# A selective scan on one Trainium2 core: state sums and gate one unit later, softplus operations behind the products, a third buffer for the scan's output

## The chip, the core and the metric

The kernel runs on one core of a Trainium2 chip. The core has five engines that take their instructions in order, each from a queue of its own: PE (matrix products into PSUM), DVE (vector), ACT (activation functions), POOL (GpSimd, vector operations on SBUF alone here) and SP, which in this stage issues the DMA transfers. An instruction starts when those ahead of it on its engine are out of the way and the semaphores that it waits for have come. The metric is the device time of one execution in microseconds (us); the median of several executions counts.

## The reference

A tensor of 2 x 192 x 96 x 96 floats goes through four layers, each of the form x + layer(groupnorm(x)). The change touches the last, a selective state-space scan over 9216 positions of each of the two images, with 384 inner channels and 16 states per channel:

```python
xz = x_flat @ W_in.T
x_in, z_gate = jnp.split(xz, 2, axis=-1)
x_conv = jax.nn.silu(conv4(x_in) + conv_b)          # a causal filter of 4 taps per channel
dt, B_ssm, C_ssm = jnp.split(einsum('bdl,kd->blk', x_conv, W_x), ...)
delta = jax.nn.softplus(dt @ W_dt.T + b_dt + b_dt)
A = -jnp.exp(A_log)
def step(h, inp):
    u_t, d_t, B_t, C_t = inp
    dA = jnp.exp(d_t[..., None] * A)
    h = dA * h + (d_t * u_t)[..., None] * B_t[:, None, :]
    y_t = jnp.einsum('bdn,bn->bd', h, C_t)
    return (h, y_t)
y = (ys + D * x_conv) * jax.nn.silu(z_gate)
out = x + einsum('bdl,cd->bcl', y, W_out)
```

(`conv4` stands for the grouped convolution; the rest is cut.)

## The kernel before

The last layer is the function `layer3`; it takes the last 3.2 ms of the span. The positions of an image are cut into **steps**: 17 of 511 positions (called whole) and two of 265 and 264, 19 per image and 38 in all. The 384 channels x 16 states of a step are worked on in 12 **units**, called q0 to q11 here: three blocks of 128 channels (i) by four groups of 32 channels (v), a unit being 32 channels x 16 states in a tile of 128 partitions x 4 rows. In the profile's terms, unit k of a whole step is made of these operations:

- SP loads `bu` (L2336, 1022 KB, delta times u, repeated over the states) from a DRAM buffer `ud`; ACT copies the state into its column 0 (L2340).
- POOL multiplies `bu` by the B row (`times_b`, L2346).
- PE spreads delta over the states into four PSUM banks `da` (`steps_of`, L2356), ACT makes exp(A * delta) of each in place (`decay`, L2370). There are five such banks, so that only one of the next unit's four can be filled before the present scan has let go of the others.
- DVE runs the recurrence, four scans into `h` (`scan`, L2379); ACT keeps the last column (`keep`, L2386).
- Products with the C row: DVE does three of the four rows of `h` into `hc` (`times_c`, L2403), POOL the fourth into `hp` (`times_c_aside`, L2414).
- PE adds the 16 states up in a PSUM bank `acc` (`sum_of`, L2427). The first unit of every four starts the bank with D times u (the `skip` product, L2421), and after the fourth DVE multiplies by the gate (`gate`, L2440, into `y`), which frees the one `acc` bank.

Work for coming steps is put between the units by generators that advance at set places. `early(s + 2)` projects (L2242), filters (L2262) and activates; it starts in q3, does its first product in q5 and its last in q10, and SiLU on ACT in q11. `late(s + 1)` makes B, C and delta: product L2278 in q0, L2303 in q1 and q2, softplus as |.|, exp, +1 and log on ACT with one subtraction on DVE (L2313, with the log L2314 in q4) and three operations on POOL: L2316 in q5, L2318 in q6, L2320 in q7. L2320 makes `du`, which four DMAs (L2322) write to `ud`, from which all twelve `bu` of the next step are loaded. `output(s - 1)` (L2452, L2460) fills q3 to q5. All these products go through one PSUM bank `pe`, so each waits until the one before has been copied out.

The order on PE, ACT, DVE and POOL is that of the loop `for k in range(nk)` (L2496), written out by hand; only SP's queue is put in order by the compiler's scheduler. In an iteration k PE gets: products of a generator that runs ahead (q1, q7, q8, q9), `sum_of(k - 2)`, `steps_of(k + 1)`, products of a generator that runs behind. ACT: `decay(k + 1)`, the copies of those products, the state copies. DVE: `scan(k)`, additions of `output`, `times_c(k)`, `gate(k - 2)`, the softplus subtraction. POOL: the softplus operation if there is one, `times_c_aside(k - 1)`, `times_b(k + 2)`. SP: among others `load(k + 3)`.

Buffers: `bu` has four; `hc`, `hp`, `us` and `zs` three (pool `s3`); `h`, `xt`, `dl` and the rows of B and C two (pool `sb`); `xn`, `xi`, `du`, `ln`, `y`, `xr` one (pool `s1`). Tile waits are put in by the framework: with two buffers `scan(k)` waits until all readers of `h` of unit k - 2 are done.

Of the kernel before, what the change touches and what calls it, by code (L numbers as in the profile page):

```python
# [6 lines left out]
F32 = mybir.dt.float32  # L7
# [11 lines left out]
P = 128  # L19
CH = 96  # L20
# [38 lines left out]
def halves(ap):  # L59

    return ap.rearrange("(k p) t -> p k t", k=2)


class Net:
# [2021 lines left out]
    def layer3(self, x, out, stats):  # L2086
# [4 lines left out]
        TM = 511  # L2091
# [4 lines left out]
        NV = 4  # L2096
# [3 lines left out]
        with ExitStack() as ctx:  # L2100
            wp = ctx.enter_context(tc.tile_pool(name="w3", bufs=1))
            s1 = ctx.enter_context(tc.tile_pool(name="l3s", bufs=1))
            sb = ctx.enter_context(tc.tile_pool(name="l3", bufs=2))
            s3 = ctx.enter_context(tc.tile_pool(name="l3h", bufs=3))
# [102 lines left out]
            steps = []  # L2207
# [8 lines left out]
            def bank(T):  # L2216
                return ps.tile([P, TM], F32, name="pe")[:, :T]

            def early(s):

                b, t0, T = steps[s]
                xt = sb.tile([CH, 2, TM], F32, name="xt")[:, :, :T]
                nc.sync.dma_start(out=xt, in_=halves(x[b])[:, :, t0 : t0 + T])
                xn = s1.tile([CH, 2, TM], F32, name="xn")[:, :, :T]
                gs, gb = gns[b]
                for k in range(2):
                    nc.scalar.activation(
                        xn[:, k], xt[:, k], AF.Identity, bias=gb[:, k : k + 1], scale=gs[:, k : k + 1]
                    )
                us = s3.tile([P, ND, TM], F32, name="us")[:, :, :T]  # L2230
                zs = s3.tile([P, ND, TM], F32, name="zs")[:, :, :T]
                xi = s1.tile([P, ND, TM + 3], F32, name="xi")[:, :, : T + 3]
                got[s] = {"us": us, "zs": zs}
                if t0 == 0:
                    nc.gpsimd.memset(tail, 0.0)
                nc.scalar.copy(xi[:, :, 0:3], tail)
                yield

                def project(at):
                    pe = bank(T)  # L2240
                    for k in range(2):
                        nc.tensor.matmul(  # L2242
                            pe, w_in[:, k, at : at + P], xn[:, k], start=k == 0, stop=k == 1
                        )
                    return pe

                for d in range(ND):
                    pe = project(d * P)
                    yield
                    nc.scalar.copy(xi[:, d, 3:], pe)  # L2250
                    if d == ND - 1:
                        nc.scalar.copy(tail, xi[:, :, T : T + 3])
                    yield
                for d in range(ND):
                    pe = project(DI + d * P)
                    yield
                    nc.scalar.copy(zs[:, d], pe)  # L2257
                    yield
                for d in range(ND):
                    pe = bank(T)  # L2260
                    for j in range(4):
                        nc.tensor.matmul(  # L2262
                            pe, taps[:, d, j], xi[:, d, j : j + T], start=j == 0, stop=j == 3
                        )
                    yield
                    nc.scalar.activation(us[:, d], pe, AF.Identity, bias=cb[:, d : d + 1])
                    yield
                nc.scalar.activation(zs, zs, AF.Silu)
                nc.scalar.activation(us, us, AF.Silu)
                yield  # L2270
# [57 lines left out]
            def where(k):  # L2328
                return k // NQ, k % NQ, k % NQ // NV, k % NV
# [13 lines left out]
            def times_b(k):  # L2343
                s, q, _, _ = where(k)
                bu = got[s]["bu", q][:, :, 1:]
                nc.gpsimd.tensor_tensor(  # L2346
                    bu, bu, got[s]["bs"].unsqueeze(1).to_broadcast([P, 4, steps[s][2]]), ALU.mult
                )
# [17 lines left out]
            def decay(k):  # L2366
                s, q, _, _ = where(k)
                for r in range(4):
                    da = got[s]["da", q][r][:, 1:]
                    nc.scalar.activation(  # L2370
                        da, da, AF.Exp, scale=nA[:, 4 * q + r : 4 * q + r + 1]
                    )

            def scan(k):
                s, q, _, _ = where(k)
                h = sb.tile([P, 4, TM + 1], F32, name="h")[:, :, : steps[s][2] + 1]
                bu = got[s]["bu", q]
                for r in range(4):
                    nc.vector.tensor_tensor_scan(  # L2379
                        h[:, r], got[s]["da", q][r], bu[:, r], 0.0, ALU.mult, ALU.add  # L2380
                    )
                got[s]["h", q] = h
# [5 lines left out]
            def rows_c(s):  # L2388
                cc = ps.tile([P, TM], F32, name="cc")[:, : steps[s][2]]
                nc.tensor.matmul(  # L2390
                    cc,
                    pick.rearrange("p n e -> p (n e)"),
                    got[s]["xd"][:NST],
                    start=True,
                    stop=True,
                )
                got[s]["cc"] = cc
# [19 lines left out]
            def sum_of(k):  # L2417
                s, q, i, v = where(k)
                if v == 0:
                    acc = ps.tile([P, TM], F32, name="acc")[:, : steps[s][2]]  # L2420
                    nc.tensor.matmul(  # L2421
                        acc, skip[:, i], got[s]["us"][:, i], start=True, stop=False
                    )
                    got[s]["acc"] = acc
                acc = got[s]["acc"]
                for r in range(4):
                    nc.tensor.matmul(  # L2427
                        acc[32 * r : 32 * r + 32],
                        gather[:, v],
                        got[s]["hc", q][:, r] if r < 3 else got[s]["hp", q],  # L2430
                        start=False,
                        stop=v == NV - 1,
                        tile_position=(0, 32 * r),
                    )

            def gate(k):
                s, q, i, v = where(k)
                if i == 0:
                    got[s]["y"] = s1.tile([P, ND, TM], F32, name="y")[:, :, : steps[s][2]]
                nc.vector.tensor_tensor(  # L2440
                    got[s]["y"][:, i], got[s]["acc"], got[s]["zs"][:, i], ALU.mult
                )
# [26 lines left out]
            nk = ns * NQ  # L2469
# [23 lines left out]
            def go(name):  # L2493
                next(running[name], None)

            for k in range(nk):  # L2496
                s, q, _, _ = where(k)
                if q == 0 and s + 1 < ns:
                    running["late"] = late(s + 1)
                if q == 2 and s:  # L2500
                    running["out"] = output(s - 1)
                if q == 3 and s + 2 < ns:
                    running["early"] = early(s + 2)
                if q in AHEAD:
                    go(AHEAD[q])
                    go(AHEAD[q])
                if k >= 2:
                    sum_of(k - 2)
                if q == 0 and s:
                    rows_c(s)  # L2510
                scan(k)
                if q in (4, 5):
                    go("out")
                if k + 1 < nk:
                    steps_of(k + 1)
                if q in BEHIND:
                    go(BEHIND[q])
                if k + 1 < nk:
                    decay(k + 1)
                if q in BEHIND and BEHIND[q] != "out":  # L2520
                    go(BEHIND[q])
                if q == 3:
                    go("late")
                    go("early")
                times_c(k)
                if k >= 2 and (k - 2) % NV == NV - 1:
                    gate(k - 2)
                if q in (4, 5, 6, 7):
                    go("late")
                if q == 11:  # L2530
                    go("early")
                if k:
                    times_c_aside(k - 1)
                if k + 2 < nk:
                    times_b(k + 2)
                if k + 3 < nk:
                    load(k + 3)
                keep(k)
            sum_of(nk - 2)
            times_c_aside(nk - 1)  # L2540
            sum_of(nk - 1)
            gate(nk - 1)
            for _ in output(ns - 1):
                pass
# [93 lines left out]
```

## Time and profile before

| what | value |
|---|---|
| median of 3 runs | 10368.99 us (10358.51 to 10370.72) |
| the profiled execution | 10352.81 us |
| its span in the trace | 10351.0 us |
| mean granted PE clock over the span | 0.915 |
| one whole step (q0 to q0, first start of L2403) | 86.28, 89.68 and 87.22 us (three in a row, from 9029.57 us on) |
| busy in the first of these three | PE 81.08, DVE 78.62, POOL 79.71, ACT 54.90 us |
| first and last L2403 of the layer | 7139.6 and, in the last step's first unit, 10300.4 us |

Busy time is the time in which an engine has an instruction in execution; for PE it contains waits in its pipeline, and matmuls that run side by side in different quarters of the array overlap. A line of the waits view reads: engine and line that waited, what it waited for, total us, times, longest. In a timeline each row is one group of instructions: start, duration, engine, line, operation, and in brackets the idle time ahead of it with what ended it. "x4" is four instructions merged in one row.

### The profile page before, as it was taken

How to read it: one execution, taken by the hardware profiler on the slowest of the kernel's cores; microseconds unless marked ns; L12 is line 12 of the kernel's file. 1: busy time of each engine (PE TensorE's matmuls, PEld its weight loads, DVE VectorE, ACT ScalarE, POOL GpSimd, SP SyncE). 2: the span in 40 equal slices, each digit the busy share in tenths (PEclk: the TensorE clock that was granted, in tenths of full speed). 3: DMA queues.
4: the chain of work that ended last, by engine and by line, in shares of the span. 5: the costliest groups of instructions: out<-in, count | busy, mean ns of one | idle time of the engine just before them, and what ended most of it. 6: DMA issues, size and time to landing. Idle time of an engine off the chain costs nothing. (4 is left out here: it accounts for less than half of the span.)

```text
span 10351.0 us, 222379 instructions
## 1 busy us (share of the span) xinstructions
PE 9158.5 (88%) x87686; PEld 5342.5 (52%) x87686; DVE 8210.6 (79%) x8842; ACT 6081.6 (59%) x11850; POOL 6980.6 (67%) x5645
## 2 busy tenths in 40 slices
PE   4799999999979999999866777887999999999998
PEld 3587788787768888888722222223222222222223
DVE  5688878788677777777655789984889888888888
ACT  0366666666667677777500168664666666666665
POOL 1466666766666666666511268773888889988898
PEclk8899999999989999999978788887999999988898
DMA  8455555555434555555444344433787777878776
GB/s 148 91 139 135 136 136 139 137 136 134 119 90 128 136 136 138 139 137 138 109 131 129 117 149 159 130 118 83 172 176 172 172 174 173 173 173 172 174 170 149
DMA packets 877164, 1465.17 MB, mean 142 GB/s; under 512 B 251616, under 2 KB 682276, under 8 KB 875012
## 3 DMA queue, kind: packets, MB, share of 16 engines
q1 hardware_dynamic: 663276, 1264.09, 48.9%
q0 software_dynamic: 104000, 133.19, 5.8%
q10 hardware_dynamic: 108840, 53.57, 2.1%
q8 instruction: 701, 11.49, 0.5%
q14 instruction: 347, 2.84, 0.1%
HBM read 871.06 MB, written 381.46 MB: 121 GB/s over the span
## 5 line engine op out<-in xcount | busy, mean ns | idle before, releaser
L2379 DVE TENSOR_TENSOR_SCAN h<-da,bu 128x512 f32<-128x512 f32 (+2 forms) x1824 | 1981.6, 1148 | 374.0 <-POOL hp L2414 200.1
L581 DVE TENSOR_TENSOR sp<-h 128x2304 f32<-128x2304 f32 x790 | 2165.0, 2773 | 41.6 <-ACT h L560 41.6
L2346 POOL TENSOR_TENSOR bu<-bu,bs 128x2044 f32<-128x2044 f32 (+2 forms) x456 | 1958.3, 4295 | 66.0 <-DMA bu<-ud 53.0
L605 ACT COPY st<-pt 128x512 f32<-128x512 f32 (+1 forms) x2370 | 1213.6, 515 | 1100.8 <-PE pt L597 1029.4
L597 PE MATMUL pt<-ident,sp 128*128 128x128 f32 x14220 | 1674.8, 276 | 87.4 <-DVE sp L581 41.0
L603 DVE COPY st<-pt 128x512 f32<-128x512 f32 x1580 | 1063.7, 687 | 829.9 <-PE pt L597 810.7
L597 PEld LDWEIGHTS pt<-ident,sp 128*128 128x128 f32 x14220 | 1565.3, 142 | 169.9 <-issue 97.2
L551 POOL TENSOR_TENSOR h<-u,step 128x1152 f32<-128x1152 f32 (+1 forms) x474 | 1096.0, 2330 | 679.8 <-DVE u L524 480.8
L569 POOL DMA_DIRECT2D xw<-xp_d x2500 | 1389.9, 619 | 194.7 <-PE pt L648 82.5
L2370 ACT ACTIVATE da<-da,nA 128x511 f32<-128x511 f32 (+2 forms) x1824 | 1063.4, 638 | 595.0 <-PE da L2356 586.9
L648 PE MATMUL pt<-st,xw 64*32 64x288 f32 (+1 forms) x30000 | 1098.0, 371 | 141.8 <-DVE st L603 62.7
L674 ACT COPY val<-pt 128x288 f32<-128x288 f32 (+1 forms) x3000 | 958.0, 404 | 285.2 <-PE pt L648 259.9
L776 PE MATMUL pf<-main,wd 126*64 126x128 f32 (+1 forms) x17064 | 986.2, 274 | 9.7 <-DMA far_m<-val 9.4
L776 PEld LDWEIGHTS pf<-main,wd 126*64 126x64 f32 x17064 | 913.7, 140 | 155.9 <-issue 146.9
L2356 PE MATMUL da<-dl,spread 32*128 32x511 f32 (+2 forms) x3648 | 984.0, 643 | 6.7 <-DVE h L2379 6.7
L648 PEld LDWEIGHTS pt<-st,xw 64*32 64x32 f32 x30000 | 548.0, 107 | 556.6 <-ACT val L674 171.7
L2403 DVE TENSOR_TENSOR hc<-h,cc 128x1533 f32<-128x1533 f32 (+2 forms) x456 | 751.2, 1647 | 0.0
L797 PE MATMUL pf<-more,wl 118*64 118x144 f32 (+5 forms) x11592 | 737.9, 278 | 3.0 <-DMA more<-far_l 2.2
L797 PEld LDWEIGHTS pf<-more,wl 118*64 118x64 f32 (+1 forms) x11592 | 670.2, 137 | 71.1 <-issue 63.4
L2356 PEld LDWEIGHTS da<-dl,spread 32*128 32x128 f32 x3648 | 311.6, 192 | 674.7 <-DVE h L2379 396.1
L2414 POOL TENSOR_TENSOR hp<-h,cs 128x511 f32<-128x511 f32 (+2 forms) x456 | 553.4, 1214 | 99.6 <-DVE h L2379 48.1
L2242 PE MATMUL pe<-xn,sb_w_in 96*128 96x511 f32 (+2 forms) x912 | 527.1, 709 | 94.6 <-ACT xi L2250 37.1
(344 smaller groups left out, 13016.1 us busy)
## 6 DMA issues: line engine op xcount, KB each, us to landing
bu<-ud SPq DMA_DIRECT2D x408, 1022.0 KB
main<-val SPq DMA_DIRECT2D x2016, 91.1 KB
far_l<-val SPq DMA_DIRECT2D x288, 324.0 KB
xw<-xp_d POOLq DMA_DIRECT2D x2500, 26.0 KB
far_m<-val SPq DMA_DIRECT2D x288, 162.0 KB
half_d<-hv SPq DMA_DIRECT2D x54, 768.0 KB
hv<-half_d SPq DMA_DIRECT2D x54, 768.0 KB
more<-far_l SPq DMA_DIRECT2D x576, 60.8 KB
```

Source lines behind the costliest of these rows:

```text
L551: nc.gpsimd.tensor_tensor(hs, u[:, :, 8 * KK * l : 8 * KK * l + n].unsqueeze(3).to_broadcast([P, 2, n, WS]), con["step"].unsqueeze(1).unsq ...
L569: nc.gpsimd.dma_start(out=xw[e * WN : (e + 1) * WN, i], in_=xp_d[y : y + WS, x : x + WS, e * CM // 2 : e * CM // 2 + XW],)
L581: nc.vector.tensor_tensor(sp.rearrange("p s (y x) -> p s y x", x=WS), hy.unsqueeze(3).to_broadcast([P, n, WS, WS]), hx.unsqueeze(2).to_bro ...
L597: nc.tensor.transpose(pt[:, q], sp[:, 2 * (q0 + q) : 2 * (q0 + q) + 2].rearrange("p e w -> p (e w)"), self.ident,)
L603: nc.vector.tensor_copy(st[:, q0 : q0 + m], pt[:, :m])
L605: nc.scalar.copy(st[:, q0 : q0 + m], pt[:, :m])
L648: nc.tensor.matmul(to, xw[e * WN : (e + 1) * WN, win, g * CG : g * CG + 32], sts[pair][e * WN : (e + 1) * WN].rearrange("p s (r c) -> p s ...
L776: nc.tensor.matmul(place(cv, m, 2 - t // 3, 2 - t % 3, None, 0), con["wd"][:, cv, t, m * CO : (m + 1) * CO], blocks(took, 1, rows), start= ...
L797: nc.tensor.matmul(place(cv, m, 2 * cv if alone else 1 - cv, 2 - t, h, 1 - alone,), con["wl"][lanes, slot, t, m * CO : (m + 1) * CO], bloc ...
L2346: nc.gpsimd.tensor_tensor(bu, bu, got[s]["bs"].unsqueeze(1).to_broadcast([P, 4, steps[s][2]]), ALU.mult)
L2356: nc.tensor.matmul(das[r][:, 1:], spread[at, v].rearrange("p n e -> p (n e)"), got[s]["dl"][at, i], start=True, stop=True, tile_position=( ...
L2379: nc.vector.tensor_tensor_scan(h[:, r], got[s]["da", q][r], bu[:, r], 0.0, ALU.mult, ALU.add)
```

## The change

Four edits, all in `layer3`:

1. `h` comes from the pool with three buffers, `xt` (a step's input tile) from the pool with one.
2. `sum_of` is called for unit k - 3 and no longer for k - 2, at the same place of the iteration; at the end the last three units are summed after the loop.
3. `gate` goes with it: it is called for k - 3, so in q2, q6 and q10 instead of q1, q5 and q9. The `skip` product, which belongs to `sum_of`, moves from q2, q6, q10 to q3, q7, q11.
4. In q5, q6 and q7 the generator `late` advances after `times_c_aside(k - 1)` and `times_b(k + 2)`, no longer ahead of them. What is issued there is L2316, L2318 and L2320 on POOL and the four DMAs to `ud`. In q4 it stays where it was.

On SP, the scheduler's order differs in one place: the load of `xr` (L2448), which stood two `bu` loads behind the `ud` writes, now stands just ahead of them; the writes stand between the same two `bu` loads (of units q10 and q11) in both kernels.

```diff
-                xt = sb.tile([CH, 2, TM], F32, name="xt")[:, :, :T]
+                xt = s1.tile([CH, 2, TM], F32, name="xt")[:, :, :T]
...
-                h = sb.tile([P, 4, TM + 1], F32, name="h")[:, :, : steps[s][2] + 1]
+                h = s3.tile([P, 4, TM + 1], F32, name="h")[:, :, : steps[s][2] + 1]
...
-                if k >= 2:
-                    sum_of(k - 2)
+                if k >= 3:
+                    sum_of(k - 3)
...
                 times_c(k)
-                if k >= 2 and (k - 2) % NV == NV - 1:
-                    gate(k - 2)
-                if q in (4, 5, 6, 7):
+                if k >= 3 and (k - 3) % NV == NV - 1:
+                    gate(k - 3)
+                if q == 4:
                     go("late")
                 if q == 11:
                     go("early")
                 if k:
                     times_c_aside(k - 1)
                 if k + 2 < nk:
                     times_b(k + 2)
+                if q in (5, 6, 7):
+                    go("late")
                 if k + 3 < nk:
                     load(k + 3)
                 keep(k)
-            sum_of(nk - 2)
             times_c_aside(nk - 1)
-            sum_of(nk - 1)
+            for k in range(nk - 3, nk):
+                sum_of(k)
             gate(nk - 1)
```

## The prediction, made before the changed kernel had run

> **What bounds the kernel now.** I read the busy times of whole steps first, then the waits of the last layer, then the timelines of three consecutive steps, A (from 9029.57 us), B (from 9115.85) and C (from 9205.53). The steps repeat with lengths near 86.3, 89.7 and 86.9 us, mean 87.6. In each, DVE works 78.6 to 78.9 us, so about 9 us of a step are DVE idle time; that is all there is to gain. The last whole step, which prepares nothing for a successor, takes 78.2 us: DVE alone. The waits of the layer (waiter, releaser, total, times, longest):
>
> ```profile
> POOL ln L2316 <- ACT bu L2340: 217.6, 36, 8.4
> ...
> DVE h L2379 <- POOL hp L2414: 194.0, 86, 4.0
> ...
> DVE h L2379 <- ACT da L2370: 128.1, 133, 4.4
> ```
>
> The second line is the scan waiting for its buffer, which POOL still reads for `hp`; over the 36 steps with softplus work, 5.4 us each. The third is the scan waiting for decays. POOL's timeline in step A shows where the second comes from (L2346 is `bu` of q6, then softplus, `hp` of q4, `bu` of q7, softplus, `hp` of q5):
>
> ```profile
> 9052.49 4.52 POOL L2346 TENSOR_TENSOR bu<-bu,bs 128x2044 f32<-128x2044 f32 x1 [0.79 <-ACT du L2310]
> 9062.12 3.42 POOL L2316 TENSOR_TENSOR ln<-ln,du 128x1533 f32<-128x1533 f32 x1 [5.12 <-ACT bu L2340]
> 9065.49 1.28 POOL L2414 TENSOR_TENSOR hp<-h,cs 128x511 f32<-128x511 f32 x1
> 9066.72 4.51 POOL L2346 TENSOR_TENSOR bu<-bu,bs 128x2044 f32<-128x2044 f32 x1
> 9071.18 3.44 POOL L2318 TENSOR_TENSOR dl<-dl,ln 128x1533 f32<-128x1533 f32 x1
> 9074.57 1.27 POOL L2414 TENSOR_TENSOR hp<-h,cs 128x511 f32<-128x511 f32 x1
> ```
>
> POOL stands idle 5.12 us for the logarithm (ACT ends L2314 at 9062.04) with `hp` of q4 queued behind. That unit's scan ended at 9056.40. From there POOL needs 3.4 + 1.2 + 4.5 = 9.1 us a unit against 6.1 of DVE, and the scans of q7 and q8 start when `hp` ends:
>
> ```profile
> 9075.88 4.57 DVE L2379 TENSOR_TENSOR_SCAN h<-da,bu 128x512 f32<-128x512 f32 x4 [2.14 <-POOL hp L2414]
> 9080.36 1.73 DVE L2403 TENSOR_TENSOR hc<-h,cc 128x1533 f32<-128x1533 f32 x1
> 9084.95 4.57 DVE L2379 TENSOR_TENSOR_SCAN h<-da,bu 128x512 f32<-128x512 f32 x4 [2.86 <-POOL hp L2414]
> ```
>
> In B three scans wait, 0.67 + 2.87 + 2.86 us. But from q6 on a second chain runs almost as late, through PE and ACT by way of the one bank `pe` and the decays: product, decay of four, copy, next product. PE in step A:
>
> ```profile
> 9065.41 3.77 PE L2242 MATMUL pe<-xn,sb_w_in 96*128 96x511 f32 x4 [0.58 <-DVE xr L2460]
> 9068.98 1.91 PE L2421 MATMUL acc<-us,skip 128*128 128x511 f32 x2
> ...
> 9073.23 1.98 PE L2242 MATMUL pe<-xn,sb_w_in 96*128 96x511 f32 x4
> 9076.27 1.98 PE L2242 MATMUL pe<-xn,sb_w_in 96*128 96x511 f32 x4 [1.06 <-ACT xi L2250]
> ```
>
> The first product takes 3.77 us where the same product later takes 1.98, and `skip` 1.91 instead of 1.02: PE comes out of a spell of waiting at a lower rate. The view of the chain that ended last goes the same way, PE, ACT, PE, from 9065.41 to the scan of q11, and not through DVE.
>
> **The changes, by this profile.** No instruction is added or removed; everything is order and waits.
>
> *Third `h`, softplus behind the products.* In A after: POOL does `hp` of q4 at 9057.0, as soon as it is free. Then `bu` of q7, whose load is issued when the scan of q3 ends (9050.3). The load of q6 was issued at 9044.23 and landed at 9052.49, 8.3 us; so `bu` of q7 runs from 9059.2 to 63.7 (shifted by the gate, below), L2316 63.7 to 67.1, then 5.7 + 3.4 + 5.7 + 3.4: L2320 ends at 85.4, against 83.7 now. All `hp` come before the scan that needs them, with units to spare: the waits of 194 us go wholly. POOL's idle time for the logarithm goes too, filled by `hp` and `bu`.
>
> *Gate.* 0.68 us of DVE moves from q1 to q2 and q5 to q6. The scan of q2 waits for decays anyway in B and C; so q3 to q5 start 0.68 later and the first projection too: 9066.1 in A. *Skip:* off the PE chain in q6, where it runs at 1.91, into q7 at 1.02; from q10, where it stands in the chain with 1.0, to q11, where it is in the chain too. Sum 0 but for the slow rate, which then hits the sums: I take 1.9 for the first sum (0.99 twice), where `skip` and sum together now take 3.2.
>
> *A new wait.* `hc` of unit k uses the buffer that `sum_of(k - 3)` now reads in the same iteration. In q9 that sum stands behind a filter product (9092.16 + 3.70), so DVE stalls up to 2.6 us before L2403, with the next scan queued behind. But `steps_of(k + 1)` stands right behind the sum, and its decay is ready 1.9 us after the sum's end, L2403 1.7 after: the scan waits for the decay all the same. Bounds from the rows: 0 to 2.6 us a step; I take 0, as the row of the decay ends last.
>
> *What is late next: the chain.* A, row by row: projection 66.1 to 69.9; sum to 71.8; `da` of q7 1.07; decay from 73.0 (now 73.32); copy, projection 75.95 to 77.9; `skip` and sum to 79.9; decay of q8 from 81.06; projections and sum of q8 to 86.9; `da` of q9. This one now takes 3.31 us (9086.27 to 89.58) since it is paced by the late scan of q8; after, that scan starts at 81.7, and `da` takes 1.1. The filter of q9 starts at 91.05 instead of 92.16, and all that follows up to the decay of the next q1 is 1.1 us earlier. C has the same rows (projection 3.75, `skip` 1.91, paced `da` 2.81): 1.2 us. In B the projection takes 3.08, the scans were later (9155.61, 9164.70, 9173.77), `da` of q8 is paced too (3.59), and PE fell back to its low rate in between (a projection of 3.77 at 9172.46). Same walk: scan q7 at 61.8, q8 at 68.0, q9 at 75.0, the filter of q9 at 77.35 instead of 81.85: 4.5 us.
>
> *`bu` of q11.* L2320 is later by up to 1.7 us, the `ud` writes with it, and the load of q11 stands behind them on SP, with those of the whole next step. In B the load's data came 13.4 us after L2320 ended (72.5 to 85.92):
>
> ```profile
> 9185.92 4.51 POOL L2346 TENSOR_TENSOR bu<-bu,bs 128x2044 f32<-128x2044 f32 x1 [0.79 <-DMA bu<-ud]
> ```
>
> After, in A: 85.4 + 13.0 (between B's 13.4 and at most 12.6 in A) + 4.5 = 9102.9; the chain lets the scan of q11 start at 9103.8: covered, by 0.9 us. In B: 73.2 + 13.4 + 4.5 = 91.1 against 90.7: B's gain shrinks to 4.1. The three loads behind follow at their 5 us each and are covered. `xr`, moved ahead of the writes, takes 383 KB out of the crowd after them; 0. `xt` with one buffer: its former content was read a step earlier, so 0.
>
> *Sum.* (1.1 + 4.1 + 1.2) / 3 = 2.1 us a step, 36 steps: 77 us. From the profiled 10352.8 that gives 10276; that execution lies 16.2 us under the median of 10369.0, so on the scale of the median **10292 us**, 0.7% faster.
>
> At the first projection the row (3.6 us at the low rate, then `skip` at 1.91 still at it) makes me charge 1.9 us for the first sum. The Trainium skill, "TensorE: Matmul & The Clock Gate", Part 1, says that PE runs at half rate until it has been busy for a window of about 3.4 us, and that these windows run freely. By that rule the sum could already be at the full rate in many steps, 0.9 us less, or some 24 us more gain over the A and C steps; the row shows more than 5 us at the low rate, and I keep the row. The free-running window would also account for B's 3.08; nothing in this trace shows the window itself.
>
> **Rivals.**
> 1. *All of the `hp` waits come back* because the chain speeds up as well: it is the low PE rate at 9065 that makes it late, and in B, where it was not so slow, the gain is four times that of A. If each step gains its own hp wait: 194 us, 10175. Against it: the paced `da` of q5 and q6, which leave PE idle, stay.
> 2. *Nothing moves:* the chain of A and C is everywhere, the slow sum and the 1.0 of `skip` in q7 eat the 1.1, or the stall before L2403 costs up to its 2.6 in q9. Within 21 us of the median: 10369.
> 3. *Slower: the softplus operations now stand behind `bu` of q7, which waits for its load.* In the crowd after `ud`, the load of q1 was issued at 9009.41 and its `bu` started after a DMA wait at 9022.40: 12.9 us. If the load of q7 took 12.9 instead of 8.3, L2320 would end 4.6 later, `bu` of q11 at 9107.5, where the scan of q11 now starts at 9105.3: +2.2 us a step, 79 us, 10448. It decides from a landing of 10.7 us on. Against it: in the DMA view the slices from 9028 on have gaps (down to 1 and 0 tenths busy); for it: q6's load already kept POOL waiting 0.79 us.
>
> **How the numbers follow.** Forecast 0.62, from 15 to 150 us of gain; rival 1 0.15, rival 2 0.13, rival 3 0.10. The low end of the range is most of rival 1 (10185), the high end holds rival 2 with the edge of rival 3 (10385). A measurement of this kernel can tell 0.2% (21 us) from no change. Faster by more: 0.62 and 0.15, less 0.01 at the forecast's edge: 0.76; same: 0.14; slower 0.10.
>
> **What would show it.** Right: the wait of L2379 for `hp` falls from 194 us to nearly none; that of L2316 for ACT from 218 to under 40; the wait of L2379 for the decays grows beyond 128 (the chain); a wait of POOL L2346 for DMA appears, some 3 to 5 us a step, in q11; L2403 waits for sums in q9. Steps of 84.5 to 86 us, without the 89.7. Wrong: scans that wait for `bu` (rival 3), or steps below 83 us (rival 1).

## The result and the profile after

The changed kernel is slower: 10400.51 us, median of 7 runs (10395.49 to 10411.4), against 10358.51 for the kernel before in 7 runs; ratio 1.0044, interval 1.0035 to 1.0054. I had forecast 0.7% faster, with 0.10 for slower. The profiled execution has a span of 10393.7 us, 42.7 more than before.

The waits view of the last layer, changed kernel (waiter, releaser, total us, times, longest), the lines that answer to those of before:

```profile
DVE hc L2403 <- PE acc L2427: 180.0, 143, 3.8
POOL bu L2346 <- DMA bu<-ud: 165.1, 41, 8.7
...
POOL ln L2316 <- ACT bu L2340: 90.0, 29, 3.2
ACT ln L2314 <- DVE du L2313: 75.7, 28, 7.5
...
DVE h L2379 <- ACT da L2370: 49.2, 51, 3.8
...
DVE h L2379 <- POOL hp L2414: 0.9, 1, 0.9
```

The wait that the change aimed at is gone, 194.0 us to 0.9, and the scans' wait for decays fell too. New are 180 us of L2403 waiting for the sums. By these waits alone DVE gains 193 + 79 - 180 = 92 us. Yet the whole steps (33 of them, without the last, which prepares shorter steps) take 88.8 us in the mean, against 87.7 before. What grew is not a wait. Groups by line and shape, first the kernel before, then the changed one (count, busy us, mean ns, idle before):

```profile
L2313 DVE SCALAR_TENSOR_TENSOR du<-ln,du 128x1533 f32<-128x1533 f32 x34 | 59.4, 1747 | 0.2 <-ACT ln L2311 0.2
```

```profile
L2313 DVE SCALAR_TENSOR_TENSOR du<-ln,du 128x1533 f32<-128x1533 f32 x34 | 162.6, 4783 | 0.0
```

The softplus subtraction, one instruction a step, same operands and same shape, takes 4.8 us in the mean instead of 1.75: 103 us in the whole steps, and 6 more in two of the shorter ones (128x795, 3.4 to 9.3 us for the two). It stands as busy time. DVE of the changed kernel in one step:

```profile
8371.34 1.74 DVE L2403 TENSOR_TENSOR hc<-h,cc 128x1533 f32<-128x1533 f32 x1
8373.00 5.50 DVE L2313 SCALAR_TENSOR_TENSOR du<-ln,du 128x1533 f32<-128x1533 f32 x1
8378.41 4.55 DVE L2379 TENSOR_TENSOR_SCAN h<-da,bu 128x512 f32<-128x512 f32 x4
```

and POOL at the same time:

```profile
8372.38 4.50 POOL L2346 TENSOR_TENSOR bu<-bu,bs 128x2044 f32<-128x2044 f32 x1
8380.09 3.42 POOL L2316 TENSOR_TENSOR ln<-ln,du 128x1533 f32<-128x1533 f32 x1 [3.21 <-ACT bu L2340]
```

POOL's product ends at 8376.88; L2313 ends at 8378.50, 1.62 later. It looks as if L2313 had begun to work only then. In another step of the same execution it was the other way round (here POOL's rows stand first, then DVE's):

```profile
8109.60 6.67 POOL L2346 TENSOR_TENSOR bu<-bu,bs 128x2044 f32<-128x2044 f32 x1 [0.17 <-ACT bu L2340]
8116.23 3.43 POOL L2316 TENSOR_TENSOR ln<-ln,du 128x1533 f32<-128x1533 f32 x1
```

```profile
8110.16 1.75 DVE L2313 SCALAR_TENSOR_TENSOR du<-ln,du 128x1533 f32<-128x1533 f32 x1
8111.83 4.56 DVE L2379 TENSOR_TENSOR_SCAN h<-da,bu 128x512 f32<-128x512 f32 x4
```

There L2313 is short, and POOL's product long. Of the 34 whole instructions 27 take over 5 us, six 1.75 and one 1.89. The busy times of these two steps (stretch, length, PE, PEld, DVE, ACT, POOL, clock, DMA share, GB/s):

```profile
8343.15:8431.96 88.81, 80.24 (x274) 23.50 (x272) 82.79 (x67) 54.60 (x102) 79.10 (x28) 0.88 0.77 171
8080.31:8165.46 85.15, 79.92 (x273) 23.30 (x272) 79.05 (x67) 54.42 (x102) 78.50 (x27) 0.88 0.78 176
```

3.66 us of step length, 3.74 us of DVE busy time. In the kernel before POOL stood idle beside each of the 34 whole L2313 (128x1533): it was waiting for the logarithm, which waits for L2313. The row in step A, with POOL idle from 9057.0 to 9062.12 (its row is in the prediction):

```profile
9058.56 1.75 DVE L2313 SCALAR_TENSOR_TENSOR du<-ln,du 128x1533 f32<-128x1533 f32 x1
```

The change filled that idle time with a product. One row of the kernel before already showed the two side by side. The last whole step makes delta for a shorter one, and there L2313 (128x795) met a product of POOL and took 2.41 us, where the other one of this form took 0.99:

```profile
10198.52 2.41 DVE L2313 SCALAR_TENSOR_TENSOR du<-ln,du 128x795 f32<-128x795 f32 x1
```

```profile
10195.57 4.51 POOL L2346 TENSOR_TENSOR bu<-bu,bs 128x2044 f32<-128x2044 f32 x1
```

POOL's product ends at 10200.08, L2313 at 10200.93, 0.85 later.

**Theory S:** L2313 is the layer's only regular DVE instruction with both inputs in SBUF (scans, `hc`, gate and output each read one from PSUM), and it and POOL's products exclude each other: while one of them works, the other stands still, though the profile shows it as running. **Theory W**, the rival: the new wait of L2403 for the sums, 180 us, is what costs, and the long L2313 only fills time that DVE would wait anyway.

### The profile page after: what moved, and what is told of

Read it like the earlier page. It is cut to its first block, busy times and chain, and to the rows that moved or that the text cites. A ratio compares the mean times of both kernels' runs of the same rounds, so it can differ in the third digit from the quotient of the medians.

```text
span 10393.7 us, 222647 instructions
## 1 busy us (share of the span) xinstructions
PE 9082.2 (87%) x87686; PEld 5316.3 (51%) x87686; DVE 8335.3 (80%) x8842; ACT 6073.6 (58%) x11850; POOL 6994.7 (67%) x5645
## 5 line engine op out<-in xcount | busy, mean ns | idle before, releaser
L2379 DVE TENSOR_TENSOR_SCAN h<-da,bu 128x512 f32<-128x512 f32 (+2 forms) x1824 | 1980.6, 1146 | 112.0 <-ACT da L2370 88.1
L597 PE MATMUL pt<-ident,sp 128*128 128x128 f32 x14220 | 1675.8, 276 | 85.9 <-DVE sp L581 40.1
L2356 PE MATMUL da<-dl,spread 32*128 32x511 f32 (+2 forms) x3648 | 931.2, 688 | 109.6 <-DVE h L2379 109.4
L2403 DVE TENSOR_TENSOR hc<-h,cc 128x1533 f32<-128x1533 f32 (+2 forms) x456 | 754.6, 1655 | 193.7 <-PE acc L2427 193.7
L2242 PE MATMUL pe<-xn,sb_w_in 96*128 96x511 f32 (+2 forms) x912 | 510.8, 689 | 87.7 <-ACT xi L2250 40.5
```

Of the source, the lines that this page charges most:

```text
L597: nc.tensor.transpose(pt[:, q], sp[:, 2 * (q0 + q) : 2 * (q0 + q) + 2].rearrange("p e w -> p (e w)"), self.ident,)
L2356: nc.tensor.matmul(das[r][:, 1:], spread[at, v].rearrange("p n e -> p (n e)"), got[s]["dl"][at, i], start=True, stop=True, tile_position=( ...
L2379: nc.vector.tensor_tensor_scan(h[:, r], got[s]["da", q][r], bu[:, r], 0.0, ALU.mult, ALU.add)
```

## The experiments

All ratios are to the kernel before, run on the same chip; its medians there were 10353.97 us (first four) and 10359.87 us (last four).

**1. One input from PSUM** (`e1_psum_input`; changed kernel; the instruction now computes zero, so the rounding correction of the softplus is left out).

```diff
-                nc.vector.scalar_tensor_tensor(du, ln, -1.0, du, ALU.add, ALU.subtract)
+                if s and steps[s - 1][2] >= T:
+                    cc = got[s - 1]["cc"][:, :T].unsqueeze(1).to_broadcast([P, ND, T])
+                    nc.vector.scalar_tensor_tensor(du, ln, 0.0, cc, ALU.mult, ALU.mult)
+                else:
+                    nc.vector.scalar_tensor_tensor(du, ln, -1.0, du, ALU.add, ALU.subtract)
```

> The changed kernel, but the softplus subtraction on DVE (L2313) takes its second input from a PSUM bank instead of SBUF, with the same shape and length; it then computes zero, so the rounding correction of the softplus is left out. Theory S (DVE's only instruction with two SBUF inputs and POOL's products exclude each other: L2313 went from 1.75 to 5.3 us in 28 of 36 steps): L2313 back near 1.75 us in every step, POOL's L2346 beside it still 4.5, steps near 85.2 us as in the few steps of the changed kernel where it was short; 75 us under the kernel before (ratio 0.993). Theory W (the new wait of L2403 for the sums, 180 us in total, is what costs): the wait stays, so does the time, ratio 1.004.

Measured 10290.03 us, ratio 0.9932 (0.9919 to 0.9946). The group of the instruction, now at L2315, and the waits of L2403 (now L2407) for the sums (now L2431):

```profile
L2315 DVE SCALAR_TENSOR_TENSOR du<-ln,cc 128x1533 f32<-128x1533 f32 x33 | 57.5, 1742 | 0.0
```

```profile
DVE hc L2407 <- PE acc L2431: 185.3, 142, 6.5
```

The instruction is as short as before beside the same products of POOL, the step takes 85.8 us in the mean, and the wait that W blames is as large as in the changed kernel. Between this kernel and the changed one lie 1.1% of the time, some 115 us, and 3.1 us a step; L2313 differs by 3.0 us. The edit changes where one operand lies, and the arithmetic with it; run 7 changes the place alone. The granted PE clock, 0.907 over the span of the changed kernel against 0.915 before, is 0.908 here, so it is not what costs either. S holds, W falls.

**2. Four buffers for `hc`** (`e4_hc_four`; changed kernel).

```diff
-                xn = s1.tile([CH, 2, TM], F32, name="xn")[:, :, :T]
+                xn = xt
...
-                xd = sb.tile([NBC + DTR, TM], F32, name="xd")[:, :T]
+                xd = s1.tile([NBC + DTR, TM], F32, name="xd")[:, :T]
...
-                hc = s3.tile([P, 3, TM], F32, name="hc")[:, :, :T]
+                hc = sc.tile([P, 3, TM], F32, name="hc")[:, :, :T]
```

> The changed kernel with four buffers for hc, so that L2403 no longer waits for the sum of the same iteration (room made by normalising x in place and one buffer for xd). Theory S: the 180 us of waits of L2403 for the sums vanish, but the scans wait for the decays in their place; the time stays within 20 us of the changed kernel, ratio 1.002 to 1.005, L2313 still 5.3 us. Theory W: the 100 us and more come back, ratio 0.992 to 0.995.

Measured 10411.95 us, ratio 1.0051 (1.0035 to 1.0068). The waits for the sums are gone altogether, and in their place:

```profile
DVE h L2379 <- ACT da L2370: 251.6, 188, 4.1
```

49.2 + 180.0 in the changed kernel, 251.6 here: the same lateness of PE, met one instruction later. L2313 is long in 33 of 34 here and takes 24 us more in all than in the changed kernel, so the wait may have been worth up to about that; W needs 100. W falls a second time.

**3. The softplus operations ahead again** (`e2_softplus_ahead`; changed kernel).

```diff
-                if q == 4:
+                if q in (4, 5, 6, 7):
                     go("late")
...
-                if q in (5, 6, 7):
-                    go("late")
```

> The changed kernel with the three softplus operations of POOL back ahead of the products (q5, q6, q7), all else as changed. POOL then waits for the logarithm, with nothing in execution, while DVE does L2313. Theory S: L2313 1.75 us, no scan waits for hp since h has three buffers, steps of 85 to 86 us, ratio 0.992 to 0.995. Theory W: the sums still stand before L2403, ratio 1.003 or more.

Measured 10302.96 us, ratio 0.9949 (0.9936 to 0.9963); L2313 1790 ns in the mean, steps 85.9 us. POOL's idle time for the logarithm is back (218.0 us of L2316 waiting, as before); the median is 13 us above that of run 1, where this wait is 20 us, and the intervals overlap, so a cost of it is not shown. Scans now wait for `bu`, 130.6 us in all, 114 of them in q8 and q9. In the same two units L2403 waits only 15 us for the sums, against 110 in the changed kernel: the one wait stands mostly in the place of the other.

**4. Only the first of them ahead** (`e3_first_ahead`; changed kernel).

```diff
-                if q == 4:
+                if q in (4, 5):
                     go("late")
...
-                if q in (5, 6, 7):
+                if q in (6, 7):
                     go("late")
```

> The changed kernel with only the first softplus operation (L2316, q5) back ahead of the products; the other two stay behind them. It is this one whose wait keeps POOL idle during L2313. Theory S: as with all three ahead, L2313 1.75 us, ratio 0.992 to 0.995. Theory W: 1.003 or more. If POOL's place of L2318 and L2320 (and with it the ud writes) matters, this run differs from the one with all three ahead, by up to 20 us.

Measured 10426.92 us, ratio 1.0069 (1.0056 to 1.0083): neither theory's number, though L2313 is short (1759 ns). The step found something else. POOL and DVE of this kernel, q11 of one step:

```profile
8420.22 4.53 POOL L2346 TENSOR_TENSOR bu<-bu,bs 128x2044 f32<-128x2044 f32 x1 [4.32 <-DMA bu<-ud]
```

```profile
8424.78 4.57 DVE L2379 TENSOR_TENSOR_SCAN h<-da,bu 128x512 f32<-128x512 f32 x4 [2.92 <-POOL bu L2346]
```

L2320 of this step ended at 8408.98; `bu` of q11, whose load stands behind the `ud` writes, could start 11.2 us later, and the scan of q11 waits for it, 4.6 us in the mean of 34 steps. Here POOL waits for the logarithm and then, before L2320, does one pair of products (`hp` and `bu`, 5.7 us) more than with all three operations ahead; so the writes, the load and the scan of q11 come later: L2320 ends 61.9 us after the step's start in the mean, in run 3 after 56.3. I had allowed 20 us for this place; it cost 124 against run 3. It is the thin margin of 0.9 us that the prediction gave the load of q11, overrun.

**5. The order alone** (`e5_order_alone`; kernel before, with the third hunk's move of `go("late")` in q5 to q7 and nothing else).

```diff
-                if q in (4, 5, 6, 7):
+                if q == 4:
                     go("late")
...
                     times_b(k + 2)
+                if q in (5, 6, 7):
+                    go("late")
```

> The kernel before with the softplus operations behind the products (q5 to q7) and nothing else. The gate stays in q1, q5, q9, so the softplus subtraction on DVE (L2313) starts 0.68 us earlier against POOL's next product than in the changed kernel, where POOL's began 0.6 us ahead of it in most steps. Theory S: in each step L2313 is either short (then the step is 85 to 86 us) or over 5 us (then 88 to 89); with both kinds the time lies between, ratio 0.993 to 1.004, and the long ones tell where. Theory W: no sums before L2403 here, so the gain is whole, 0.992 to 0.995, whatever L2313 takes.

Measured 10377.1 us, ratio 1.0017 (1.0007 to 1.0027). L2313 is long in 25 of 34, and takes 5.15 us in the mean of all; the whole steps with 1.75 take 84.4 to 86.6 us, the others 88.1 to 91.7. W has no place here (no sum stands before L2403), and the gain is gone all the same.

**6. The third buffer of `h` alone** (`e6_third_h`; kernel before, with the change's first two hunks and nothing else).

```diff
-                xt = sb.tile([CH, 2, TM], F32, name="xt")[:, :, :T]
+                xt = s1.tile([CH, 2, TM], F32, name="xt")[:, :, :T]
...
-                h = sb.tile([P, 4, TM + 1], F32, name="h")[:, :, : steps[s][2] + 1]
+                h = s3.tile([P, 4, TM + 1], F32, name="h")[:, :, : steps[s][2] + 1]
```

> The kernel before with three buffers for h (and one for x) and nothing else: sums and gate for k - 2, softplus ahead of the products. Theory S: POOL idle during L2313, 1.75 us; no scan waits for hp; ratio 0.992 to 0.996, like the run with all softplus operations ahead, which says that moving sums and gate is worth nothing. If the later sums are what brings the gain, this run stays within 0.2% of the kernel before.

Measured 10282.45 us, ratio 0.9924 (0.9910 to 0.9939): faster than both kernels, and the fastest median of the versions that leave nothing out, though its interval overlaps those of runs 3 and 8. Its waits:

```profile
POOL ln L2316 <- ACT bu L2340: 188.4, 36, 8.4
DVE h L2379 <- ACT da L2370: 184.9, 200, 7.0
DVE h L2379 <- POOL bu L2346: 73.1, 42, 2.9
...
DVE h L2379 <- POOL hp L2414: 0.7, 1, 0.7
```

Next to no wait for `hp`; POOL idle beside L2313 in 30 of 34 (1908 ns in the mean: in the other four POOL's product is not over yet, and they take 2.6 to 4.3 us); steps 85.4 us. Moving sums and gate gains nothing beside it; run 3, which has them moved, is 20 us behind, with intervals that overlap.

**7. `hc` from the rows in SBUF** (`e7_hc_from_rows`; kernel before, same result).

```diff
-                    got[s]["cc"].unsqueeze(1).to_broadcast([P, 3, T]),
+                    got[s]["cs"].unsqueeze(1).to_broadcast([P, 3, T]),
```

> The kernel before, but L2403 multiplies by the copy of the C rows in SBUF that POOL uses instead of the one in PSUM: the same result, twelve more instructions a step with two SBUF inputs. Theory S: they and POOL's products exclude each other, so a step needs at least POOL's 79.7 + 12 x 1.7 + 1.75 = 102 us: 10850 us or more, L2403 at 3 to 5 us, ratio 1.05 and up. If L2313 became long for another reason (its place, its length, the writes into its own input), L2403 stays at 1.7 us and the time within 1%.

Measured 10792.3 us, ratio 1.0418 (1.0398 to 1.0437). Groups of this kernel, against 4515 and 1729 ns in the kernel before:

```profile
L2346 POOL TENSOR_TENSOR bu<-bu,bs 128x2044 f32<-128x2044 f32 x408 | 2242.6, 5497 | 6.6 <-DMA bu<-ud 4.5 <-ACT da L2370 2.1
...
L2403 DVE TENSOR_TENSOR hc<-h,cs 128x1533 f32<-128x1533 f32 x408 | 1204.7, 2953 | 0.0
```

DVE and POOL of this kernel at one place:

```profile
9046.81 2.79 DVE L2403 TENSOR_TENSOR hc<-h,cs 128x1533 f32<-128x1533 f32 x1
```

```profile
9046.72 1.26 POOL L2414 TENSOR_TENSOR hp<-h,cs 128x511 f32<-128x511 f32 x1
9047.94 6.02 POOL L2346 TENSOR_TENSOR bu<-bu,bs 128x2044 f32<-128x2044 f32 x1
```

Both behave like L2313: L2403 waits out `hp`, then `bu` waits out L2403. So it is the operands and not that one instruction. I had expected 102 us a step at least and 10850; most steps take 99.9 to 100. One of them (stretch, length, PE, PEld, DVE, ACT, POOL, clock, DMA share, GB/s):

```profile
8575.77:8675.73 99.96, 91.21 (x273) 26.87 (x272) 97.08 (x68) 55.34 (x102) 96.75 (x28) 0.86 0.72 152
```

POOL's busy time of 96.75 us and its 3.21 us of waiting for the logarithm make up the step. In it nine of POOL's twelve `bu` take 6.0 us, and the other three 4.5, but ahead of each of those three stands an `hp` of 2.8 instead of 1.27: POOL loses some 1.5 us in each of the twelve units, not the whole 1.73 of L2403. I had also let POOL lose to L2313; in this step it is L2313 that loses, with 6.05 us.

**8. The softplus operations between the products** (`e9_between`; changed kernel).

```diff
                 if k:
                     times_c_aside(k - 1)
+                if q in (5, 6, 7):
+                    go("late")
                 if k + 2 < nk:
                     times_b(k + 2)
-                if q in (5, 6, 7):
-                    go("late")
```

> The changed kernel with the softplus operations between the two products of POOL: behind hp, ahead of bu. POOL waits for the logarithm after hp and has nothing in execution during L2313. Theory S: L2313 1.75 us, ratio 0.992 to 0.995, at best 0.002 under the run with all softplus operations ahead, since hp comes earlier and the ud writes no later. Theory W: 1.003 or more.

Measured 10304.66 us, ratio 0.9943 (0.9928 to 0.9958), L2313 1971 ns. L2313 is short (under 1.8 us) in 27 of 34; the others met the end of an `hp` or `bu`. So what matters is that POOL has nothing in execution during L2313, not where exactly it waits. Nothing is gained on run 3.

## Why the prediction was wrong

- **The step that failed** is "Third `h`, softplus behind the products": "POOL's idle time for the logarithm goes too, filled by `hp` and `bu`." I counted the filling of that time as free. DVE was in L2313 during it: in step A its row stands from 9058.56, 0.68 later with the gate moved, and my own times put `bu` of q7 from 9059.2 to 63.7. The run with one operand in PSUM shows that this is where the 1.1% went. I had introduced the sum with "No instruction is added or removed; everything is order and waits", and so took every duration from rows of the kernel before. In the rows of L2313 that I priced by, POOL did no work: 1.75 us in each of the 34 of whole steps, always within an idle time of POOL of 4.9 to 8.4 us. The one row in which the two met, 2.41 us at 10198.52, I did not look at: it stands in the step that I had called the last, "which prepares nothing for a successor". That reading was wrong; the step prepares shorter ones, and its softplus is in the trace. With 3.0 us more a step for L2313 the forecast of 2.1 less becomes 0.9 more, 33 us, against 42 measured.
- **The rest of the sum held.** Without the exclusion the change is worth 0.68% (run 1), forecast 0.7%; steps of 85.8 us, forecast 84.5 to 86. Its usual step is 85.3 us, so steps like A, B and C are 1.0, 4.4 and 1.6 us shorter, forecast 1.1, 4.1 and 1.2; a single one of 89.6 is left. The first sum behind the slow projection, charged with 1.9 us, takes 1.5 to 1.9 in the 17 steps of run 1 that I read, so the 0.9 us less that I had thought possible did not come. And the sum had set the moved sums and the gate at 0 but for that charge; run 6 shows that the gain needs neither.
- **The new wait at 0** was right in its price, though it shows 180 us and in q1, q7, q8 and q9 rather than q9 alone: run 2 took it away and was no faster; the 24 us more of L2313 there are what a gain could hide behind. One sign of it was read wrongly. I expected the wait for the decays to grow beyond 128; it fell to 49, because the wait for the sum now stands ahead of it; in run 2, without that wait, it is 251.6.
- **`bu` of q11:** POOL's wait for that load is there as forecast (156 of the 165 us are in q11, 4.3 a step, said 3 to 5) and nearly covered, with 0.4 us a step of scans waiting. The thin margin was real: run 4 moved L2320 later and paid for it.
- **L2316's wait** fell to 90 us, not under 40: the long L2313 makes the logarithm late. In run 1, with L2313 short, it is 20.
- **Rival 3** (slower by way of the load of q7) ended on the right side by luck: POOL waited for that load in five steps only, 3.5 us in all, and the scans of q11, where the cost would have shown, waited 0.4 us a step, not 2.2.

The Trainium skill has the rule, "SBUF — State Buffer", section "Who interferes with whom": a DVE instruction with at most one SBUF input (outside the two-port modes) does not contend with GpSimd, and one with two SBUF inputs contends with a GpSimd instruction that reads SBUF. Section "SBUF: two separate sides" of the same page adds that the one that starts first has the port pair for the whole instruction and that the other fully blocks. Runs 1 and 7 agree with both halves of it: 1.74 us against 4.8 for one operand moved, and 1.73 against 2.95; the blocking lasted 1.51 us of an instruction of 1.73. I did not weigh it. The trace of before had one row that called for it, the 2.41 us at 10198.52.

## What to carry to other kernels

Idle time on one engine can be what keeps an instruction of another short. Before filling it, list what runs beside it and where its operands lie: here both DVE instructions that were tried with two inputs in SBUF (L2313, and L2403 in run 7) and POOL's products shut each other out for most of the other's duration, and the profile books that as busy time, not as a wait. Look for one line whose duration differs between rows of the same form; a group's mean can hide it. Where a wait for a buffer is the loss, try the buffer alone first: here it was worth 0.76% by itself, and the reordering that came with it cost more than that.

## What was not expected of the hardware

- The exclusion works both ways, for most of an instruction: L2313 1.75 to 5.3 us and more, POOL's product 4.51 to 6.67. The 7.05 us of one whole step are two losses in a row: L2313 was shut out by an `hp` recorded 0.34 us ahead of it, and then by the `bu` behind it, recorded 0.89 us after the start of L2313.
- If the loser needs its usual time from where it begins to work, it begins 0.13 to 0.15 us before the recorded end of the other: L2313 at 8376.75 (`bu` ends at 8376.88), `bu` of run 7 at 9049.45 (L2403 ends at 9049.60). This is worked out from the rows, not seen.
- The recorded starts do not settle who goes first when they are close. With POOL's product recorded 0.51 and 0.56 us ahead, L2313 still won (1.75 us) in two steps; with 0.09 and 0.24 it lost. From 0.6 us on POOL's `bu` always won in this execution.
